# A two-layer decoder on one core: the opening's products reordered, pieces of a planned order moved, and each attention's two output halves added at once

## The chip, the cores and the metric

The kernel runs on one core of a Trainium2 chip. The metric is the time of one execution in microseconds (us) on the device; lower is better. Engines are named as in the profile: PE is TensorE (matrix products and transposes), PEld its weight loads, DVE is VectorE, ACT is ScalarE, POOL is GpSimd, SP is SyncE, which issues most of the DMA transfers. All data is float32.

## The reference

A decoder of two layers on `x` of shape (8, 256, 256): 8 sequences of 256 rows, 256 wide. Each sublayer is added to its input.

```python
x = x + L0_attn(layernorm(x))            # 16 heads of 16, rotary, biases bq bk bv bo
x = x + L0_xattn(ctx, layernorm(x), b, seq_len)   # keys and values: halves of ctx; bias b, mask by length; no projections
x = x + L0_ffn(layernorm(x))             # expert choice, see below
x = x + L1_attn(layernorm(x))            # 16 heads of 16, rotary, causal, no biases
x = x + L1_xattn(layernorm(x), ctx)      # 16 heads of 64, one learned key and value more
x = x + L1_ffn(layernorm(x))             # top-1 of 8 experts of width 704, and a shared one
```

The change touches the first four. The feed-forward of layer 0 (`B` sequences of `N` = 256 rows, `E` = 8 experts, `M` = 32 rows for each) is:

```python
t = log(clip(x @ gate_w, 1e-6))                       # (B, N, E)
for _ in range(8):                                    # Sinkhorn
    t = t - logsumexp(t, axis=-2); t = t - logsumexp(t, axis=-1)
vals, idx = top_k(swapaxes(exp(t), -1, -2), M)        # each expert chooses 32 rows of a sequence
routed = x[b, idx]                                    # gathered
out = zeros_like(x).at[b, idx].set((routed @ experts) * vals)   # a row chosen twice: one of the entries stays
```

## The kernel before

**Units and steps.** All of `x` stays in the core's memory. The first 465 us are 24 units, in the order in which they stand in the list `units`: for each pair of sequences b, b+1 of layer 0 two self attentions (units 4i and 4i+1) and two cross attentions (4i+2 and 4i+3), then the eight causal self attentions of layer 1 (units 16 to 23). A unit has four steps k, one for each half of the heads and half of the keys. Behind the units come layer 1's cross attention, its experts and the end, where the program has nothing to do with the change.

In step k of unit n the main loop issues, in this order: `scores(k + 1)` (the next step's scores: PE `st` at L334, two exps on ACT at L345, each of half the tile, and in layer 1 a causal mask on POOL for each, L350); the planned pieces marked EARLY; `values(k)` (PE `o`, L371; at odd k also the division on DVE, L387 to L397: `by_q`, `dens`, `att`, `attT`); and the other planned pieces of this step, sorted by a due number. `beside(n, k, at, piece)` puts a piece into that plan. Within these 465 us the order of each engine's instructions is this order of issue (`manual_schedule`): an instruction that waits holds all that stand behind it on its engine.

The on-chip banks for PE's results are few: one tile of four banks for the scores (so `st` waits until both exps of the step before have read it), one bank for `o`, and three banks in rotation, tag `mm`, for all else: `tr` (transposes), `qk`, `v`, `qps`/`qpsx` (queries transposed), `ao`/`oR` (outputs), `lg`, `cs`, `vps`, `cps`, `rps`, `y`, `back`.

**A self attention's pieces.** `stats` (DVE statistics, `lnrs` on POOL, L258), `norm` (`xn`, L262, on POOL; on DVE for the first two units), `rows` (four transposes `tr` of `xn` on PE, copy `xnT` on ACT, L294), `heads(0)` and `heads(1)` (`qk` for half of the rows: L282 on PE, rotary `qc`, `qs` on DVE at L402 and L418, in layer 0 the bias on POOL at L457, and for half 0 the sum `qkr` on POOL, L459), `joined` (that sum for half 1, on DVE, L463), `vals(0)`, `vals(1)` (`v` on PE, `padv` on ACT), `begin` (transposes of `qkr`, `qps`, and their copies `kT` and `qm` on ACT), and after the unit `biased` (POOL, layer 0) and `out(0)`, `out(1)`: `ao` of 128 rows in a bank of its own on PE, and an add of 256 columns to `x` on DVE (L492) each.

**A cross attention's pieces.** `vals` (POOL copies), `stats`, `norm` (`xnx`, DVE), `begin` (`qpsx` on PE at L547), `out` (`oR`, four transposes at L557, one add of 512 columns, L559).

**The expert choice.** `chosen_experts(b0, 2)` is a generator for two sequences, four of them (entries 0 to 3), and each `next` issues one piece: stats and norm (`xnb` on POOL) of both, two transposes, two gate products `lg` (with a maximum on DVE), eight rounds `cs` (column sums on PE, then five DVE operations of some 0.2 us, L661 to L668; the next round's product needs the last of them), `vps` and the search for the 32 largest (DVE), the DMAs through `slots` in memory back to `idx_row` and `by_half`, `cps` (two transposes of `by_half`, L698, a copy `col` on DVE and `pick` on POOL, L709), then for each sequence `rps` (gather as a product), `y` (experts; with `put` on POOL and L739 to L756 on DVE: two accumulations, the weight, and `ys`) and `back` (scatter as a product) with an add to `x` (L765). The tables `pieces` (entries 0 and 1), `sooner` (entry 2) and `soonest` (entry 3) say where each of them goes: (units after the pair's first, step, due number), with 4i + 4 added for entry i.

**The opening.** The first two self attentions stand before the loop. PE's order there: xn of the first transposed, its qk(0), v(0), qk(1), v(1), transposes of `qkr`, `qps`, the first `st`; then the second's transposes and qk(0), the second `st`.

**Two more rules.** `norm` of units 20 and 22 comes in step (n - 2, 1), before the `values` there, for other units of layer 1 in (n - 3, 3). In step (20, 1) POOL issues the loads of the weights of layer 1's cross attention. Behind unit 23 its outputs and the tables `wn` and `nvw` of that cross attention follow.

Of the kernel before, what the change touches and what calls it, by code (L numbers as in the profile page):

```python
# [29 lines left out]
F32 = mybir.dt.float32  # L30
# [4 lines left out]
ALU = mybir.AluOpType  # L35
# [4 lines left out]
P = 128  # L40
B, S, D = 8, 256, 256
# [16 lines left out]
PINNED = {mybir.EngineType.PE, mybir.EngineType.DVE, mybir.EngineType.Activation, mybir.EngineType.Pool, mybir.EngineType.SP}  # L58
# [99 lines left out]
def plain(  # L158
# [4 lines left out]
    nc = tc.nc  # L163
# [6 lines left out]
    x = const.tile([P, NT, D], F32, name="x")  # L170
# [90 lines left out]
    def normed(dst, src, mv, rs, i, engine=nc.vector):  # L261
        return engine.tensor_scalar(dst, src, mv[:, i, 0:1], rs[:, i : i + 1], ALU.subtract, ALU.mult)  # L262
# [11 lines left out]
    def product(out, lhsT, rhs, start, stop):  # L274
        return [
            nc.tensor.matmul(out[h], lhsT[:, h], rhs, start=start, stop=stop, skip_group_check=True)  # L276
            for h in (slice(0, 64), slice(64, P))
        ]

    def product4(out, lhsT, rhs, start, stop):  # L280
        for h in range(0, P, HP):
            nc.tensor.matmul(  # L282
                out[h : h + HP], lhsT[:, h : h + HP], rhs, start=start, stop=stop, skip_group_check=True
            )
# [114 lines left out]
    def rotary(qk, t, layer, work):  # L399

        qc = work.tile([P, 2 * H, HD], F32, tag="qc", name="qc")
        nc.vector.tensor_tensor(  # L402
            qc,
            qk.rearrange("p (h d) -> p h d", d=HD),
            cos[:, t, :].unsqueeze(1).to_broadcast([P, 2 * H, HD]),
            ALU.mult,
        )
        qs = work.tile([P, 2 * H, HD], F32, tag="qs", name="qs")
        if layer == 0:
            of = "p (h i s) -> p s h i"  # L410
            src, dst = qk.rearrange(of, s=2, i=HD // 2), qs.rearrange("p h (i s) -> p s h i", s=2)
            sn = sin0[:, t, :].rearrange("p (i s) -> p s i", s=2)
        else:
            of = "p (h s i) -> p s h i"
            src, dst = qk.rearrange(of, s=2, i=HD // 2), qs.rearrange("p h (s i) -> p s h i", s=2)
            sn = sin1[:, t, :].rearrange("p (s i) -> p s i", s=2)
        for s in range(2):
            nc.vector.tensor_tensor(  # L418
                dst[:, s],
                src[:, 1 - s],  # L420
                sn[:, s, :].unsqueeze(1).to_broadcast([P, 2 * H, HD // 2]),
                ALU.mult,
            )
        return qc.rearrange("p h d -> p (h d)"), qs.rearrange("p h d -> p (h d)")

    class SelfAttention:
# [10 lines left out]
        def norm(self):  # L437
            self.xn = work.tile([P, 2, D], F32, tag="xn", name="xn")
            for t in range(2):
                self.head = normed(  # L440
                    self.xn[:, t, :], x[:, 2 * self.b + t, :], self.mv, self.rs, t, nc.gpsimd if self.n else nc.vector
                )

        def rows(self):
# [38 lines left out]
                    xt = x[:, 2 * self.b + t, :]  # L483
                    nc.gpsimd.tensor_tensor(xt, xt, self.bias[1], ALU.add)

        def out(self, t):
            b, attT = self.b, self.core.attT
            xt = x[:, 2 * b + t, :]
            ps = mm.tile([P, 2 * D], F32, tag="mm", name="ao")[:, :D]
            for c in range(2):  # L490
                product4(ps, attT[:, c, bass.ts(t, P)], self.wo[:, c, :], c == 0, c == 1)
            nc.vector.tensor_tensor(xt, xt, ps, ALU.add)  # L492

# [5 lines left out]
    def key_tables():  # L501
        tok_i = const.tile([P, 2], I32, name="tok_i")
        nc.gpsimd.iota(tok_i, [[P, 2]], base=0, channel_multiplier=1)
        nc.vector.tensor_copy(tokid, tok_i)
        seq = const.tile([P, B], F32, name="seq")
        nc.vector.tensor_copy(seq, seq_i)
        alive = const.tile([P, B], F32, name="alive")
        nc.vector.tensor_scalar(alive, seq, 1.0, None, ALU.is_ge)
        for t in range(2):
            hid = small.tile([P, B], F32, tag="hid", name="hid")  # L510
            nc.vector.tensor_scalar(hid, seq, tokid[:, t : t + 1], -1.0e12, ALU.is_le, ALU.mult)
            nc.vector.scalar_tensor_tensor(kbias[:, :, t], hid, keyb[:, t : t + 1], alive, ALU.add, ALU.mult)
        nc.vector.tensor_tensor(
            mask2a,
            mask2.unsqueeze(1).to_broadcast([P, B, 2]),
            alive.unsqueeze(2).to_broadcast([P, B, 2]),
            ALU.mult,
        )
# [47 lines left out]
    mm = banks.enter_context(tc.tile_pool(name="amm", bufs=3, space=PSUM))  # L566
# [7 lines left out]
    def turn():  # L574
        for t in range(2):
            qc, qs = rotary(bs[:, :2, :].rearrange("p i d -> p (i d)"), t, 0, work)
            nc.vector.tensor_tensor(turned[:, t, :], qc, qs, ALU.add)
# [191 lines left out]
    units = []  # L769
# [80 lines left out]
    def beside(n, k, at, *made):  # L850
        plan.setdefault((n, k), []).append((at, made))
# [7 lines left out]
    EARLY = 0  # L859
    for n, u in enumerate(units):  # L860
        if u.__class__ is SelfAttention:
            u.n = n
            if n in (20, 22):
                beside(n - 2, 0, 80, u.stats)
                beside(n - 2, 1, EARLY, u.norm)
            else:
                beside(n - 3, 2, 80, u.stats)
                beside(n - 3, 3, EARLY, u.norm)
            beside(n - 2, 2, 30, u.rows)
            beside(n - 2, 3, 30, partial(u.heads, 0))  # L870
            beside(n - 1, 0, 30, partial(u.heads, 1))
            beside(n - 1, 1, EARLY, u.joined)
            beside(n - 1, *((2, 30) if u.layer == 0 and n % 4 else (1, 30)), partial(u.vals, 0))
            beside(n - 1, 1, 60, u.begin)
            beside(*((n, 0, 40) if u.layer else (n - 1, 2, 31) if n % 4 else (n - 1, 3, 40)), partial(u.vals, 1))
            beside(n, 3, 80, u.biased)
            for t in range(2):
                beside(n + 1, *((2 + t, 40) if u.layer else (0, 20 + t)), partial(u.out, t))
        else:
            beside(n - 1, 0, 80, u.stats, u.vals)  # L880
            beside(n - 1, 1, EARLY, u.norm)
            beside(n - 1, 1, 60, u.begin)
            beside(n + 1, *((2, 40) if n % 4 == 2 else (0, 20)), u.out)
    beside(0, 2, 40, add_up)
    beside(2, 2, 85, slot_keys)
    beside(3, 2, 50, slot_tables)

    begun = (-1, 2, 80), (0, 0, EARLY), (0, 1, 80)
    start = begun + (
        (0, 2, EARLY), (0, 3, 40), (0, 3, 41), (1, 0, 70), (1, 2, 70),  # L890
        (1, 3, 70), (2, 0, 15), (2, 1, 5), (2, 2, 10), (2, 2, 70), (2, 3, 70), (3, 0, 70), (3, 1, 45),
        (3, 2, 70), (3, 3, 85),
    )
    pieces = start + (
        (4, 1, 85), (4, 2, EARLY), (4, 3, 70), (5, 1, 10), (5, 2, 10), (5, 3, 10), (5, 3, 20), (6, 1, 10), (6, 2, 15),
    )
    sooner = start + (
        (4, 1, 84), (4, 1, 85), (4, 3, 20), (5, 0, 50), (5, 1, 35), (5, 2, 20), (5, 2, 50), (5, 3, 50), (6, 0, 50),
    )
    soonest = begun[:2] + (  # L900
        (0, 0, 80), (0, 1, EARLY), (0, 1, 65), (0, 1, 66), (0, 2, 50), (0, 2, 51),
        (0, 3, 60), (1, 0, 45), (1, 1, 10), (1, 1, 70), (1, 2, 70), (1, 3, 35), (1, 3, 70), (2, 0, 35),
        (2, 0, 70), (2, 1, 85), (2, 2, EARLY), (2, 2, 85),
        (3, 0, 10), (3, 0, 50), (3, 1, 35), (3, 2, 35), (3, 2, 50), (3, 3, 35), (4, 0, 50),
    )
    ex = [chosen_experts(2 * i, 2) for i in range(B // 2)]
    for i, made in enumerate(ex):
        for n, k, at in (pieces, pieces, sooner, soonest)[i]:
            beside(4 * i + 4 + n, k, at, partial(next, made, None))

    for u in units[:2]:
        u.n = 0
        u.stats()
        u.norm()
        if u is units[0]:
            opening = ExitStack()
            opening.enter_context(tc.issue_after(u.head.ins))
            order = ExitStack()
            order.enter_context(tc.manual_schedule(engines=PINNED))
            turn()  # L920
            u.rows()
            u.heads(0)
            u.vals(0)
            u.heads(1)
            u.joined()
            u.vals(1)
            for v in units[:2]:
                v.load()
        else:
            units[0].begin()  # L930
            units[0].core.scores(0)
            u.rows()
            u.heads(0)
            key_tables()
    for n, u in enumerate(units):
        if n == 1:
            expert_tables()
# [22 lines left out]
                wd, ctxs, wproj, wkv_x, wq_x, wout_x, nkrow, nvcol, lns, lnb = weights_x()  # L960
        opening.close()
    order.close()
    for t in range(2):
        units[-1].out(t)
    wn, nvw, hot8 = tables_x(wd, wq_x, wout_x, nkrow, nvcol)
    first.close()
    banks.close()
# [1 line left out]
    mm = banks.enter_context(tc.tile_pool(name="xmm", bufs=3, space=PSUM))  # L969
# [1878 lines left out]
```

## Time and profile before

| what | value |
|---|---|
| three executions | 1214.85, 1215.27, 1216.22 us; median 1215.27 |
| the profiled execution | 1214.46 us, of it 1212.7 us between the first and the last instruction |
| mean granted clock of PE | 0.992 of full speed |
| ACT, exps of layer 0's self and layer 1's attentions (L345) | 128 of 128 x 1024 or less, 0.917 us each |
| POOL, causal mask (L350) | 64 of 128 x 512, 0.671 us each |
| POOL, lnrs (L258) | 48, 0.732 us each |
| DVE, add of 256 columns (L492) | 0.42 us |
| DVE, add of 512 columns (L559, L765) | 0.69 us |
| xn pair on POOL (L262) | 2.42 us |
| xn pair on DVE (L262) | 0.73 to 0.86 us |

In the rows of the timeline the columns are: start in us from the beginning of the span, duration (first start to last end, where several like instructions are drawn together), engine, line, operation, output and inputs by the program's names, shape, number of instructions, and in brackets how long the engine had stood idle before it and what ended that. The granted clock is given as a share of full speed.

### The profile page before, as it was taken

What the parts mean: (1) busy time and instruction counts of PE and PEld (TensorE: products, weight loads), DVE (VectorE), ACT (ScalarE), POOL (GpSimd) and SP (SyncE); (2) the same over time, 40 slices, a digit from 0 to 9 for tenths busy, and PEclk for the clock granted to TensorE, in tenths of its full rate; (3) what the DMA queues carried; (4) which work ended last, traced back from release to release, by engine and by line L of the source; (5) the groups of instructions that cost most, each with busy time, mean ns of one, the idle gap of its engine ahead of it and who ended that gap; (6) DMA issues with size and microseconds to landing.
All of it is one profiled execution on the core that took longest, in us unless ns stands there. A gap on an engine that the chain in (4) does not pass through costs nothing.

```text
span 1212.7 us, 31559 instructions
## 1 busy us (share of the span) xinstructions
PE 1141.0 (94%) x13596; PEld 707.9 (58%) x13596; DVE 562.4 (46%) x1564; ACT 447.6 (37%) x696; POOL 417.2 (34%) x482
## 2 busy tenths in 40 slices
PE   5798989998999998999999999999999999999997
PEld 2344435444444445566666676666666486888874
DVE  4455767758775746223332433333335474222113
ACT  2666655656434361223232323232323131222220
POOL 2335344443746741132333323241416105000004
PEclk9999999999999999999999999999999999999999
DMA  7036232050200410010101010101012108599934
GB/s 223 1 127 205 91 117 91 2 171 2 83 2 11 167 71 2 18 37 18 37 19 37 18 37 19 37 19 37 19 37 72 36 2 322 217 399 404 386 123 138
DMA packets 51446, 116.76 MB, mean 96 GB/s; under 512 B 8273, under 2 KB 36417, under 8 KB 46945
## 3 DMA queue, kind: packets, MB, share of 16 engines
q1 hardware_dynamic: 45120, 98.90, 23.9%
q0 software_dynamic: 3456, 12.73, 2.9%
q10 hardware_dynamic: 2720, 3.02, 0.7%
q8 instruction: 109, 1.79, 0.6%
q14 instruction: 41, 0.33, 0.1%
HBM read 104.00 MB, written 27.93 MB: 109 GB/s over the span
## 4 chain that ended last, share of the span: by engine, by line
PE 73%; POOL 8%; DVE 7%; issue 6%; ACT 3%; DMA 2%; SPq 0%; POOLq 0%; ACTq 0%; DVEq 0%
PE h L276 7%; PE k L276 6%; PE v L276 6%; PE wo L276 5%; PE ox L1458 5%; PE stx L1419 4%; PE out L1836 4%; PE out L1653 3%; PE st L334 3%; PE h L1041 3%; PE o L371 3%; PE qk L282 3%; PE q L276 3%; PE tr L291 2%; PE fm L276 2%
## 5 line engine op out<-in xcount | busy, mean ns | idle before, releaser
L345 ACT ACTIVATE pT<-st 128x1024 f32<-128x1024 f32 (+1 forms) x128 | 110.5, 917 | 79.3 <-PE st L334 79.1
L371 PE MATMUL o<-pT,padv 128*32 128x256 f32 (+1 forms) x1536 | 100.4, 372 | 4.3 <-POOL pT L350 4.2
L1425 POOL TENSOR_TENSOR both<-pTx 128x512 f32<-128x512 f32 x64 | 82.1, 1310 | 50.5 <-issue 44.9
L371 PEld LDWEIGHTS o<-pT,padv 128*32 128x32 f32 x1536 | 40.9, 110 | 87.4 <-issue 41.7
L276 PE MATMUL h<-xrT,w 128*64 128x128 f32 (+1 forms) x1936 | 87.3, 250 | 3.1 <-issue 3.1
L276 PEld LDWEIGHTS h<-xrT,w 128*64 128x64 f32 x1936 | 84.7, 137 | 6.1 <-issue 3.9
L258 POOL TENSOR_TENSOR lnrs<-lnve,mhalf 128x2 f32<-128x2 f32 x48 | 35.1, 732 | 153.2 <-DVE lnve L256 141.8
L345 ACT ACTIVATE pT<-st,kbias 128x1024 f32<-128x1024 f32 x64 | 67.8, 1112 | 36.7 <-PE st L334 36.7
L1423 ACT ACTIVATE pTx<-stx 128x1024 f32<-128x1024 f32 x64 | 62.2, 1022 | 41.3 <-PE stx L1419 26.2
L1034 DVE TENSOR_TENSOR midr<-sl,h 128x128 f32<-128x128 f32 x102 | 29.4, 288 | 102.5 <-PE h L276 68.9
L334 PE MATMUL st<-qm,kT 32*128 32x512 f32 (+1 forms) x512 | 68.7, 606 | 5.2 <-ACT pT L345 3.3
L1033 ACT ACTIVATE sl<-h 128x128 f32<-128x128 f32 (+1 forms) x114 | 35.3, 310 | 97.8 <-PE h L276 58.8
L1419 PE MATMUL stx<-qTx,kTx 64*128 64x256 f32 x512 | 64.3, 391 | 2.5 <-ACT pTx L1423 2.5
L282 PE MATMUL qk<-l_wqkv,xnT 128*32 128x512 f32 x512 | 63.9, 616 | 2.2 <-ACT xnT L294 2.2
L1458 PE MATMUL ox<-pTx,vx 128*64 128x256 f32 x512 | 62.3, 385 | 0.0
L1513 POOL TENSOR_TENSOR oT<-oT,rs 128x512 f32<-128x512 f32 x30 | 37.3, 1274 | 66.7 <-DMA rs<-rd 66.7
L258 POOL TENSOR_TENSOR lxrs<-lxve,mhalf 128x2 f32<-128x2 f32 x8 | 5.6, 702 | 154.3 <-DVE sc L1172 123.3
L1419 PEld LDWEIGHTS stx<-qTx,kTx 64*128 64x128 f32 x512 | 46.1, 186 | 20.3 <-ACT pTx L1423 7.2
L276 PE MATMUL wo<-wout_x,oT 128*64 128x256 f32 x512 | 58.0, 379 | 0.0
L350 POOL TENSOR_SCALAR_AFFINE_SELECT pT<-pT 128x512 f32<-128x512 f32 x64 | 42.1, 671 | 39.3 <-ACT pT L345 39.3
L1458 PEld LDWEIGHTS ox<-pTx,vx 128*64 128x64 f32 x512 | 33.9, 136 | 26.4 <-issue 12.1
L1466 DVE COPY oT<-ox 128x512 f32<-128x512 f32 x16 | 11.1, 691 | 81.0 <-PE ox L1458 81.0
(361 smaller groups left out, 2195.1 us busy)
## 6 DMA issues: line engine op xcount, KB each, us to landing
w<-packs SPq DMA_DIRECT2D x22, 1408.0 KB
w<-packs SPq DMA_DIRECT2D x22, 768.0 KB
rs<-rd SPq DMA_DIRECT2D x16, 512.0 KB
packs<-L_ffn_w_eDF SPq DMA_DIRECT2D x8, 704.0 KB
packs<-L_ffn_w_eDF SPq DMA_DIRECT2D x8, 640.0 KB
packs<-L_ffn_w_eFD SPq DMA_DIRECT2D x8, 640.0 KB
ctxT<-ctx_T SPq DMA_DIRECT2D x8, 512.0 KB
wkv_x<-L_xattn_Wkv POOLq DMA_DIRECT2D x1, 4096.0 KB, 14.0
```

Of the source, the lines that this page charges most:

```text
L258: nc.gpsimd.tensor_tensor(rs[:, :n], ve[:, :n], mhalf[:, :n], ALU.pow)
L276: nc.tensor.matmul(out[h], lhsT[:, h], rhs, start=start, stop=stop, skip_group_check=True)
L282: nc.tensor.matmul(out[h : h + HP], lhsT[:, h : h + HP], rhs, start=start, stop=stop, skip_group_check=True)
L334: nc.tensor.matmul(st[:, r, :, :n], self.kT[rows, c, bass.ts(kt, P)], self.qm[rows, :, c, q0:], start=True, stop=True,)
L345: nc.scalar.activation(pT[:, :, :, :n], st[:, 2 * k : 2 * k + 2, :, :n], AF.Exp, scale=self.scale, **kb)
L350: nc.gpsimd.affine_select(out=pT[:, :, :, :P], in_=pT[:, :, :, :P], compare_op=ALU.is_ge, fill=0.0, base=0, pattern=[[0, 2], [0, 2], [1, P ...
L371: nc.tensor.matmul(o[HP * j : HP * j + HP, m, q0:], self.v_pad[:, kt, 8 * c + 2 * j + m, :], pTs[j // 2][:, j % 2, m, : S - q0], start=kt ...
L1419: nc.tensor.matmul(st[:, g, kt, :], kT[rows, c, bass.ts(kt, P)], qT[rows, c, :], start=True, stop=True)
L1423: nc.scalar.activation(pT, st, AF.Exp, scale=scale)
L1425: nc.gpsimd.tensor_tensor(both, pT[:, :, 0, :], pT[:, :, 1, :], ALU.add)
L1458: nc.tensor.matmul(o[XD * g : XD * (g + 1), i, :], v[:, kt, 2 * (c2 + i) + g, :], pT[:, g, kt, :], start=kt == 0, stop=kt == 1, skip_group ...
L1836: nc.tensor.matmul(ps[h], mid[:, i, h], sets[k % len(sets)][1][:, i, :], start=i == 0, stop=i == NFC - 1, skip_group_check=True,)
```

## The change

Five things are done.

1. *Opening.* PE's order becomes: xn of the first transposed, qk(0), v(0), qk(1), xn of the second transposed, v(1), transposes of the first's `qkr`, `qps`, qk(0) of the second, `st`, `st`. DVE's and POOL's order there stays.
2. *`SelfAttention.out`.* Both halves are written to one bank, and one add of 512 columns follows. In layer 1 both stand where the first one stood, in step (n + 1, 2); in layer 0 where both stood, in (n + 1, 0).
3. *Places of units' pieces.* `out` of every second cross attention goes behind heads(1) of the coming unit, in the same step; `rows` in layer 1 goes from due number 30 to 60 of its step.
4. *Table entries.* norm0 of entries 0 to 2 goes from (0, 0, EARLY) to (0, 1, EARLY), behind `joined` there. In `pieces`, `cps` goes from (4, 3) to (5, 0) and the last `back` from (6, 2) to (6, 3). In `sooner` and `soonest` several pieces go a fraction of a step or a step back.
5. *`norm` of units 20 and 22* runs on DVE in place of POOL.

The calls of `load` for the first two units that go with the old opening did nothing (they load from the third sequence on).

```diff
@@ SelfAttention.norm
-                    ..., nc.gpsimd if self.n else nc.vector
+                    ..., nc.gpsimd if self.n not in (0, 1, 20, 22) else nc.vector
@@ SelfAttention.out
-        def out(self, t):
-            b, attT = self.b, self.core.attT
-            xt = x[:, 2 * b + t, :]
-            ps = mm.tile([P, 2 * D], F32, tag="mm", name="ao")[:, :D]
-            for c in range(2):
-                product4(ps, attT[:, c, bass.ts(t, P)], self.wo[:, c, :], c == 0, c == 1)
-            nc.vector.tensor_tensor(xt, xt, ps, ALU.add)
+        def out(self):
+            attT, xb = self.core.attT, x[:, 2 * self.b : 2 * self.b + 2, :]
+            ps = mm.tile([P, 2, D], F32, tag="mm", name="ao")
+            for t in range(2):
+                for c in range(2):
+                    product4(ps[:, t, :], attT[:, c, bass.ts(t, P)], self.wo[:, c, :], c == 0, c == 1)
+            nc.vector.tensor_tensor(xb, xb, ps, ALU.add)
@@ the plan
-            beside(n - 2, 2, 30, u.rows)
+            beside(n - 2, 2, 60 if u.layer else 30, u.rows)
...
-            for t in range(2):
-                beside(n + 1, *((2 + t, 40) if u.layer else (0, 20 + t)), partial(u.out, t))
+            beside(n + 1, *((2, 40) if u.layer else (0, 20)), u.out)
...
-            beside(n + 1, *((2, 40) if n % 4 == 2 else (0, 20)), u.out)
+            beside(n + 1, *((2, 40) if n % 4 == 2 else (0, 40)), u.out)
...
-    begun = (-1, 2, 80), (0, 0, EARLY), (0, 1, 80)
+    begun = (-1, 2, 80), (0, 1, EARLY), (0, 1, 80)
...
     pieces = start + (
-        (4, 1, 85), (4, 2, EARLY), (4, 3, 70), (5, 1, 10), (5, 2, 10), (5, 3, 10), (5, 3, 20), (6, 1, 10), (6, 2, 15),
+        (4, 1, 85), (4, 2, EARLY), (5, 0, 60), (5, 1, 10), (5, 2, 10), (5, 3, 10), (5, 3, 20), (6, 1, 10), (6, 3, 10),
     )
     sooner = start + (
-        (4, 1, 84), (4, 1, 85), (4, 3, 20), (5, 0, 50), (5, 1, 35), (5, 2, 20), (5, 2, 50), (5, 3, 50), (6, 0, 50),
+        (4, 1, 84), (4, 1, 85), (5, 0, 20), (5, 0, 50), (5, 1, 35), (5, 2, 50), (5, 3, 10), (5, 3, 60), (6, 0, 50),
     )
-    soonest = begun[:2] + (
-        (0, 0, 80), (0, 1, EARLY), (0, 1, 65), (0, 1, 66), (0, 2, 50), (0, 2, 51),
-        (0, 3, 60), (1, 0, 45), (1, 1, 10), (1, 1, 70), (1, 2, 70), (1, 3, 35), (1, 3, 70), (2, 0, 35),
+    soonest = (-1, 2, 80), (0, 0, EARLY), (0, 0, 80), (0, 1, EARLY)
+    soonest += (
+        (0, 2, 35), (0, 2, 36), (0, 3, 10), (0, 3, 50),
+        (1, 0, 10), (1, 0, 70), (1, 1, 35), (1, 1, 70), (1, 2, 70), (1, 3, 35), (1, 3, 70), (2, 0, 35),
         (2, 0, 70), (2, 1, 85), (2, 2, EARLY), (2, 2, 85),
-        (3, 0, 10), (3, 0, 50), (3, 1, 35), (3, 2, 35), (3, 2, 50), (3, 3, 35), (4, 0, 50),
+        (3, 0, 70), (3, 1, 50), (3, 2, 35), (3, 3, 10), (3, 3, 35), (4, 0, 10), (4, 0, 50),
     )
@@ the opening
-    for u in units[:2]:
-        u.n = 0
-        u.stats()
-        u.norm()
-        if u is units[0]:
...
-            u.rows()
-            u.heads(0)
-            u.vals(0)
-            u.heads(1)
-            u.joined()
-            u.vals(1)
...
-        else:
-            units[0].begin()
-            units[0].core.scores(0)
-            u.rows()
-            u.heads(0)
-            key_tables()
+    first_u, second_u = units[:2]
+    first_u.stats()
+    first_u.norm()
...
+    first_u.rows()
+    first_u.heads(0)
+    first_u.vals(0)
+    first_u.heads(1)
+    first_u.joined()
+    second_u.stats()
+    second_u.norm()
+    second_u.rows()
+    first_u.vals(1)
+    first_u.begin()
+    second_u.heads(0)
+    first_u.core.scores(0)
+    key_tables()
```

More of the change, by code (lines that the diff above doesn't have):

```diff
@@ L440, in norm @@
                 self.head = normed(
-                    self.xn[:, t, :], x[:, 2 * self.b + t, :], self.mv, self.rs, t, nc.gpsimd if self.n else nc.vector
+                    self.xn[:, t, :], x[:, 2 * self.b + t, :], self.mv, self.rs, t, nc.gpsimd if self.n not in (0, 1, 20, 22) else nc.vector
                 )
@@ L909, in plain @@
             beside(4 * i + 4 + n, k, at, partial(next, made, None))
-    for u in units[:2]:
-        u.n = 0
-        u.stats()
-        u.norm()
-        if u is units[0]:
[L916 to L920, printed above, removed]
-            u.rows()
-            u.heads(0)
-            u.vals(0)
-            u.heads(1)
-            u.joined()
-            u.vals(1)
-            for v in units[:2]:
-                v.load()
-        else:
-            units[0].begin()
-            units[0].core.scores(0)
-            u.rows()
-            u.heads(0)
-            key_tables()
+    first_u, second_u = units[:2]
+    first_u.stats()
+    first_u.norm()
+    opening = ExitStack()
+    opening.enter_context(tc.issue_after(first_u.head.ins))
+    order = ExitStack()
+    order.enter_context(tc.manual_schedule(engines=PINNED))
+    turn()
+    first_u.rows()
[11 more added lines that the diff above has]
+    key_tables()
     for n, u in enumerate(units):
@@ L962, in plain @@
     order.close()
-    for t in range(2):
-        units[-1].out(t)
+    units[-1].out()
     wn, nvw, hot8 = tables_x(wd, wq_x, wout_x, nkrow, nvcol)
```

## The prediction

> **What bounds the kernel now.** I read the page's busy shares, slices and chain of waits first, then TensorE's waits by releaser up to 465 us, then the timeline around each place that the diff touches.
>
> ```profile
> PE 1141.0 (94%) x13596; PEld 707.9 (58%) x13596; DVE 562.4 (46%) x1564; ACT 447.6 (37%) x696; POOL 417.2 (34%) x482
> ...
> PE   5798989998999998999999999999999999999997
> ...
> PE 73%; POOL 8%; DVE 7%; issue 6%; ACT 3%; DMA 2%; SPq 0%; POOLq 0%; ACTq 0%; DVEq 0%
> ```
>
> PE is the bound, 94% busy. One slice is 30.3 us; the change ends with the attentions, at about 465 us, in the 16th slice. Behind that the order is the old one and PE has 9 in all slices but the last, so whatever is won or lost before 465 us arrives whole at the end. It can only come from PE's idle time, and that stands here:
>
> ```profile
> PE st L334 <- ACT pT L345: 8.5, 8, 1.5
> PE tr L291 <- DVE xn L262: 7.9, 1, 7.9
> PE tr L291 <- DVE qkr L463: 7.8, 7, 1.7
> PE cps L698 <- DMA by_half<-slots: 6.8, 3, 2.9
> PE qpsx L547 <- DVE xnx L262: 4.3, 4, 1.1
> PE o L371 <- POOL pT L350: 4.2, 5, 1.6
> PE back L282 <- DVE ys L756: 3.0, 2, 1.5
> ```
>
> Columns: total us, times, longest. A wait of PE costs more than its length:
>
> ```profile
> 171.60 0.32 PE L698 MATMUL cps<-ident,by_half 4*128 4x4 f32 x2 [2.16 <-DMA by_half<-slots]
> 171.73 2.10 PE L334 MATMUL st<-qm,kT 32*128 32x512 f32 x8
> 173.76 1.68 PE L371 MATMUL o<-pT,padv 128*32 128x256 f32 x16
> ...
> 303.19 1.97 PE L371 MATMUL o<-pT,padv 128*32 128x256 f32 x16 [1.62 <-POOL pT L350]
> 305.09 1.12 PE L557 MATMUL oR<-ident,attT 128*128 128x128 f32 x4
> 306.13 2.90 PE L282 MATMUL qk<-l_wqkv,xnT 128*32 128x512 f32 x16
> ```
>
> After 2.16 us of waiting the st takes 2.10 instead of 1.14 (as st at 28.25 below) and o 1.68 instead of 1.07: 1.57 lost beyond the wait. After 1.62 us (303.19) o, oR and qk lose 0.90 + 0.46 + 1.00 = 2.4 against their usual 1.07, 0.66 and 1.90. In both places the granted clock of the 10 us is 0.83. After the 1.68 us before cps at 375.38 and the 1.48 before back at 204.13 nothing slows. So I price a new PE wait of 2 us or more at its length plus 1.6, bounds 0 and 2.4.
>
> **The change, part by part** (plus is slower; the sum is made on the profiled execution, 1214.46 us).
>
> *Opening.* PE's old order: qk and v of the first attention, its qkr transposes and qps, st(0), then the second's transposes of xn and its qk. In the new one the transposes of the second's xn stand before v(1). DVE's order is unchanged, and it makes that xn last:
>
> ```profile
> 21.53 0.73 DVE L262 TENSOR_SCALAR xn<-x,lnmv,lnrs 128x256 f32<-128x256 f32 x2 [0.82 <-POOL lnrs L258]
> ...
> 21.76 2.09 PE L334 MATMUL st<-qm,kT 32*128 32x512 f32 x8 [1.41 <-ACT qm L313]
> ...
> 28.25 1.14 PE L334 MATMUL st<-qm,kT 32*128 32x512 f32 x8
> ```
>
> PE, which began v(1) at 16.41, now waits from about there to 21.9, some 5.4 us; v(1), the qkr transposes and qps are queued behind the waiting transposes. From 22.3: half a pair of transposes 0.5, v(1) at half clock 1.9, four qkr transposes 1.0, qps 0.6, the second's qk 1.9: st(0) at 28.2 (was 21.76). Its first exps no longer lie behind qk, so st(1) follows them: 1.14 + 1.94 later, 31.4 against 28.25, +3.15. The second's rotary is ahead, though, so the 1.50 us that PE waited for its qkr at 36.05 mostly goes: −1.2. **+1.9**; bounds +0.5 (v, transposes and qps keep full clock, 1.45 less) and +3.5 (nothing regained).
>
> *Outputs in one bank.* PE does the same products. DVE adds 512 columns once (0.69, by the row of L559) instead of 0.42 twice, but the chain add, statistics, lnrs, xnx, qpsx now begins with 0.69 in place of the last 0.42: +0.27 at the four places where PE waits for xnx (52.01, 66.54, 113.11, 127.87; 1.0 to 1.1 each): **+1.1**. In the third and fourth group rps or y products lie between and hide it; uncovered it would be 1.1 more, which is the upper bound; −0.6 the lower, if two freed semaphores and a bank do more than that.
>
> *Cross output behind heads(1), norm0 behind joined.* POOL's xnb pair (2.42) no longer stands before the rotary's bias add (L457, 1.27) of the unit's second half, which PE awaits through qkr: waits of 0.57 (98.02), 1.36 (161.67) and 1.34 (235.51) go: **−3.3**, bounds 0 and −3.3. Late next would be the xnb transposes; their place is a step or more away.
>
> *cps one step later.* Table entries 0 and 1: cps moves from just before st at 171.73 and 246.32 to behind that unit's o and ao, four us on. by_half, issued at 169.19, landed at about 171.6, well before that. Gone are 2.16 + 1.57 and 2.92 + 1.69 (st 1.75, o 1.94, ao 2.12 there against 1.14, 1.07, 1.91); cps itself, formerly hidden in the wait, adds 0.13 each: **−8.1**. Behind cps on its engines, col (DVE) and pick (POOL, 1.84) have until rps, one step later. The lower bound of the gain is 6.8 − 1.7 = 5.1, the two waits alone; the upper 8.3.
>
> *back1 one step later.* PE's 1.48 us for ys goes, at 204.13 and 278.80. But back's 1.93 us were also what covered the next chain: cs4 (206.58) needs five DVE operations (1.1 us) of the cs3 round, which queue on DVE behind the two accumulations, weight and ys up to 204.3. Without back, PE passes the four transposes and stands from 203.25 until 205.6, about 2.3 us. By the order of the rows heads(0) then starts at 209.4 instead of 208.79, and back adds its bit behind: +0.85 each, **+1.7** for both, bounds −2 and +3.
>
> *Layer 1 (units 16 to 23).* Entry 2's y0, rps and back and entry 3's pieces move half a step to a step; rows come later. Two waits arise: rps0 for pick, which POOL does behind L459 and both masks (326.2 to 328.25, 2.05), and in unit 17 cs for a chain that now stands behind y0's DVE work (335.5 to 337.4, 1.9). Two go: POOL xn of units 20 and 22 (0.93 each at 365 and 411; the pair is 2.42 on POOL, 0.73 to 0.86 on DVE), and most of the 1.68 at cps, 375.38. By the rows PE is 2.5 early at 404.5. In unit 21 POOL is rid of xn of 22 before the weight triggers, PE gets to st(21.1) at 413.4 instead of 419.33, but its o then waits for POOL's own stream (lnrs 0.73, masks 1.24, xn of 23 2.48, three lnrs 2.02, L459 1.27, masks 1.68): 421.6 instead of 425.59. Net **−4.0**, bounds −6 (POOL free, st's gain kept) and +1.5 (both waits longer, gain at 375 lost).
>
> *End.* ao doubled before st(23.0) delays exp by 0.62; the last add and nvw come 0.5 sooner: **+0.1**, bounds −1 and +1.
>
> Sum: 1.9 + 1.1 − 3.3 − 8.1 + 1.7 − 4.0 + 0.1 = −10.6.
>
> *Clock after the new waits.* cs4 twice (2.3 us; 0.7 x 1.6 = 1.1 each), rps0 and cs in layer 1 (2.0; half of 1.6 each), o of unit 21 (3 us, 1.3 since POOL binds there): 2.2 + 1.6 + 1.3 = **+5.1**.
>
> Result −5.5: 1209.0 on the profiled execution. That execution stands 0.8 below the median of 1215.27, so **1209.8 us**.
>
> [...]
>
> **Rivals.**
> (a) *No clock loss.* The same waits, but none of the five falls so that the clock drops. For it: 1.48 and 1.68 us cost nothing; against it: 2.16, 2.92 and 1.62 all did. 1215.27 − 10.6 = 1204.7.
> (b) *Wash.* The gain at the xnb places and in layer 1 is half, the rest as forecast: PE just meets the next chain (the o that waits for POOL's masks, five times now, 4.2 us). −5.5 + 1.65 + 2.0 = −1.9, and +1.6 if the opening regains nothing: 1213.4 to 1215.0.
> (c) *Slower: clock drops eat the gain.* The five new waits each cost 2.4 beyond their length, as after 303.19 (+12.0), and the opening reaches its upper bound (+1.6): −10.6 + 13.6 = +3.0, 1218.3. It decides from 2.1 per wait on (10.6 : 5), with the opening as forecast. Against it: four waits out of five would have to meet the dearer row.
> (d) *The change doesn't remove the DMA wait*: by_half is late again, because SP issues it after more transfers. In the trace slots' reads go out ahead of memk, and the order on SP isn't touched. The two waits' 5.1 on the forecast: 1214.9.
>
> **How the numbers follow.** Two executions of this kernel can be told apart from about 0.2% (2.4 us) on; that puts "the same" at 1212.8 to 1217.7. Chances: forecast 0.42 (1206.5 to 1212.5), (a) 0.18, (b) 0.14, (c) 0.20, (d) 0.06. Faster: 0.40 of the forecast, all of (a) and 0.02 of (b), 0.60. The same: 0.02 of the forecast, 0.12 of (b) and all of (d), 0.20. Slower: (c), 0.20. The range reaches a little beyond (a)'s time at the bottom and to (c)'s at the top, and leaves out the farther halves of both, 0.19: 1203.5 to 1218.3; the forecast's own is 1206.5 to 1212.5.
>
> **What would show it.** cps without a wait for by_half in units 9 and 13, and the following st at 1.14; a wait of some 5 us of PE for xn at 16.5 and st(1) near 31; cs waiting about 2.3 us for g in units 10 and 14; no wait at the qkr transposes of units 5, 9, 13; o of unit 21 waiting for POOL. I am wrong if the opening loses more than 3.5 us, if cps merely waits at its new place, or if the 10-us windows around the new cs waits show clocks of 0.83 more often than three times.

## The result: no change, and the profile after

The changed kernel takes 1215.03 us (median of 12, 1212.86 to 1217.11), the kernel before, beside it, 1215.74 (12 runs, 1208.77 to 1219.43). The ratio is 1.0002, with a 95% interval of 0.9989 to 1.0014 (the quotient of the two medians is 0.9994; either says that nothing changed). The forecast of 1209.8 is refuted in what it said: nothing was gained. The profiled execution of the changed kernel has a span of 1211.1 us at a granted clock of 0.988; before it was 1212.7 at 0.992.

First TensorE's waits up to 465 us, in the changed kernel (releaser; total us, times, longest):

```profile
PE tr L291 <- DVE xn L262: 13.1, 2, 7.6
PE st L334 <- ACT pT L345: 10.7, 8, 2.1
PE cs L282 <- DVE g L668: 8.6, 8, 2.2
PE qpsx L547 <- DVE xnx L262: 5.7, 4, 1.5
PE ao L282 <- DVE attT L397: 3.8, 1, 3.8
PE o L371 <- POOL pT L350: 3.5, 4, 1.6
PE o L371 <- DVE by_q L387: 3.2, 3, 1.2
PE tr L291 <- DVE qkr L463: 1.6, 3, 0.9
```

The waits that were to go are gone: `by_half` (6.8 before) and `ys` at `back` (3.0) stand nowhere, `qkr` fell from 7.8 to 1.6. Others are in their place, and the total hardly moved (56.4 us before, 56.0 now, up to 470 us): the second xn in the opening (+5.2), `cs` for g (8.6 against 1.1), `xnx` (5.7 against 4.3), `by_q` (3.2, new), `attT` at the end (3.8 against 2.2).

Two places, in the timeline of PE. The opening, then units 10 and 11:

```profile
20.54 1.09 PE L291 MATMUL tr<-ident,xn 128*128 128x128 f32 x4 [5.51 <-DVE xn L262]
21.56 1.93 PE L282 MATMUL v<-l_wqkv,xnT 128*32 128x256 f32 x16
23.42 1.11 PE L291 MATMUL tr<-ident,qkr 128*128 128x128 f32 x4
24.33 1.06 PE L475 MATMUL qps<-ident,qkr 128*128 128x128 f32 x4
25.32 1.94 PE L282 MATMUL qk<-l_wqkv,xnT 128*32 128x512 f32 x16
27.19 1.14 PE L334 MATMUL st<-qm,kT 32*128 32x512 f32 x8
30.39 1.14 PE L334 MATMUL st<-qm,kT 32*128 32x512 f32 x8 [2.06 <-ACT pT L345]
...
203.52 0.42 PE L282 MATMUL cs<-g,ones 128*32 128x16 f32 x16 [2.24 <-DVE g L668]
203.86 2.09 PE L334 MATMUL st<-qm,memk 32*128 32x512 f32 x8
205.88 1.94 PE L371 MATMUL o<-pT,padv 128*32 128x256 f32 x16
207.59 2.96 PE L282 MATMUL back<-ys,put 128*32 128x256 f32 x32
210.38 1.89 PE L282 MATMUL qk<-l_wqkv,xnT 128*32 128x512 f32 x16
```

PE waits 5.5 us in the opening, and v at 21.56 takes 1.93 where it took 1.04. The `cs` wait of 2.24 is followed by st 2.09 for 1.14, o 1.94 for 1.07, back 2.96 for 1.9; the granted clock from 203 to 209 us is 0.50. Such products are called half speed below.

A table made of such rows is the tool of this study. It shows how much later (+) or earlier (-) the first `st` of a step starts than in the kernel before, in us, for one profiled execution of each kernel; the experiments are told below.

| step | changed | gains only | layer 0 one bank | layer 0 one bank, two adds | layer 1 one bank | all but outputs |
|---|---|---|---|---|---|---|
| 0.3 (36.85 us) | +1.12 | -2.32 | -2.36 | -0.08 | +0.13 | +0.96 |
| 3.0 (70.75) | +2.70 | -2.32 | -0.92 | +1.56 | +0.13 | +0.97 |
| 9.0 (166.27) | +1.11 | -4.68 | -2.45 | +1.00 | -2.20 | -1.34 |
| 10.0 (185.89) | -2.36 | -8.14 | -5.92 | -1.65 | -5.67 | -4.81 |
| 11.1 (210.73) | +1.58 | -8.14 | -4.01 | -0.70 | -5.67 | -4.17 |
| 14.0 (260.55) | -4.37 | -13.97 | -9.97 | -5.71 | -11.49 | -10.12 |
| 16.0 (297.07) | -3.39 | -13.95 | -9.55 | -4.76 | -11.48 | -7.89 |
| 23.0 (445.87) | -1.62 | -13.46 | -9.50 | -4.30 | -4.87 | -9.95 |

In the changed kernel the first column falls where the forecast said (9.0 to 10.0: 3.5; 11.1 to 14.0: 6.0) and climbs in between and behind. Which part of the change makes it climb was to be tried.

### The profile page after: what moved, and what is told of

It is laid out like the page before. It is cut to its first block, busy times and chain, and to the rows that moved or that the text cites. A ratio compares the mean times of both kernels' runs of the same rounds, so it can differ in the third digit from the quotient of the medians.

```text
span 1211.1 us, 31526 instructions
## 1 busy us (share of the span) xinstructions
PE 1140.6 (94%) x13596; PEld 712.1 (59%) x13596; DVE 568.0 (47%) x1552; ACT 448.4 (37%) x696; POOL 415.4 (34%) x478
## 4 chain that ended last, share of the span: by engine, by line
PE 77%; POOL 7%; DVE 6%; issue 6%; ACT 4%; DMA 1%; SPq 0%; POOLq 0%; ACTq 0%; DVEq 0%
PE h L276 7%; PE k L276 6%; PE v L276 6%; PE wo L276 5%; PE ox L1454 5%; PE st L334 4%; PE stx L1415 4%; PE o L371 4%; PE out L1832 4%; PE out L1649 3%; PE qk L282 3%; PE h L1037 3%; PE q L276 3%; ACT pT L345 2%; PE tr L291 2%
## 5 line engine op out<-in xcount | busy, mean ns | idle before, releaser
L1462 DVE COPY oT<-ox 128x512 f32<-128x512 f32 x16 | 11.1, 691 | 81.0 <-PE ox L1454 81.0
```

## The experiments

All were timed in five rounds beside the kernel before; ratios are to it, with their intervals.

**1. The last back early again**, in the changed kernel:

```diff
-        ..., (6, 1, 10), (6, 3, 10),
+        ..., (6, 1, 10), (6, 2, 15),
```

> The changed kernel with one thing undone: the last back of entries 0 and 1 again in step (6, 2) instead of (6, 3). Theory (the moved back uncovers the Sinkhorn chain, so cs waits 2.2 us in units 10 and 14, and the half clock after the first of these costs 2.8 more): cs no longer waits, the 1.48 us before back returns, st of step 11.1 follows that of 10.2 by 15.2 us as in the kernel before instead of 19.1, and the time is 2 to 5 us under the changed kernel's, about 1211. Rival (the clock drops in any case after one of these waits, 1.5 or 2.2 alike): the rows move, the time stays at 1215.

1212.32 us, 0.9986 (0.9969 to 1.0003). The `cs` wait of 2.2 is gone and the one for `ys` is back:

```profile
203.49 1.93 PE L282 MATMUL back<-ys,put 128*32 128x256 f32 x32 [1.49 <-DVE ys L756]
205.35 0.66 PE L291 MATMUL tr<-ident,xn 128*128 128x128 f32 x4
205.94 0.32 PE L282 MATMUL cs<-g,ones 128*32 128x16 f32 x16
206.18 1.14 PE L334 MATMUL st<-qm,memk 32*128 32x512 f32 x8
207.25 1.07 PE L371 MATMUL o<-pT,padv 128*32 128x256 f32 x16
```

Nothing runs slow here. In unit 14 of this execution it was the other way round: st 1.48 behind the `ys` wait, 1.9 lost. The ratios differ by some 2 us, but their intervals overlap (0.9969 to 1.0003 here, 0.9989 to 1.0014 for the changed kernel), so the time alone doesn't show the gain. By the rows the stretches from 10.3 to 11.1 and from 14.3 to 15.1 lose 0.4 and 1.9 here against 3.9 and 1.0 in the changed kernel. It is a small part at most.

**2. cps alone one step later**, in the kernel before:

```diff
-        (4, 1, 85), (4, 2, EARLY), (4, 3, 70), (5, 1, 10), ...
+        (4, 1, 85), (4, 2, EARLY), (5, 0, 60), (5, 1, 10), ...
```

> The kernel before with one thing of the change: cps of entries 0 and 1 one step later. Theory (the by_half wait was on the path and nothing takes its place): 3.5 us less in unit 9 and 4.3 in unit 13 by the rows, about 8 us under the kernel before, 1207.5. Rival (the path behind it is set by DVE or the transfers, which catch up by unit 10): the lead at unit 9 is gone by unit 11 and the time is 1213 or more.

1207.22 us, 0.9941 (0.9918 to 0.9963): 7.2 of the 8.1 forecast, and the rows show 3.5 at unit 9 and 4.3 at unit 13. The wait for `by_half` did not move; it vanished.

**3. Layer 1 as before**, in the changed kernel: the old tables of entries 2 and 3, rows at 30 and the norm of units 20 and 22 on POOL; the single outputs stay.

> The changed kernel with entries 2 and 3, the norm of units 20 and 22 and the rows of layer 1 as before. Theory (the new order in units 16 to 21 lost 1.0 us by the rows instead of gaining 4): about 1 us under the changed kernel, 1214. Rival (my forecast: the new order gains 4 and only this execution's clock hid it): 3 to 4 us over it, 1218.5.

1219.35 us, 1.0040 (1.0023 to 1.0056): 4 to 5 us slower than the changed kernel, so my theory fell and its rival held. The new order is worth 4 to 5 us. Yet the rows of the changed kernel lose 1.8 between 16.0 and 23.0. Something else in layer 1 had to cost more than the order gains, and in this kernel only the outputs were left: from 16.0 to 23.0 it loses 7.0.

**4. Only the parts that removed waits**, in the kernel before:

```diff
-        (4, 1, 85), (4, 2, EARLY), (4, 3, 70), ...
+        (4, 1, 85), (4, 2, EARLY), (5, 0, 60), ...
-    begun = (-1, 2, 80), (0, 0, EARLY), (0, 1, 80)
+    begun = (-1, 2, 80), (0, 1, EARLY), (0, 1, 80)
-            beside(n + 1, *((2, 40) if n % 4 == 2 else (0, 20)), u.out)
+            beside(n + 1, *((2, 40) if n % 4 == 2 else (0, 40)), u.out)
```

> The kernel before with three things of the change that removed waits by the rows: cps of entries 0 and 1 later, norm0 of entries 0 to 2 behind joined, the output of every second cross attention behind heads(1). Theory (each gain is real and all others of the change give it back): 8 + 3.5 us under the kernel before, about 1204. Rival (the gains are bound to the other parts): 1210 or more.

1202.12 us, 0.9902 (0.9872 to 0.9931): 12 us faster. By the rows 11.1 us lie between 0.3 and 23.0 (second column of the table). This is the base for what follows. It was not timed again beside experiments 5 to 12; each is compared with it through the kernel before, and since the base's interval is wide, a difference between two such ratios stands within some 4 us (an estimate from the intervals).

**5. Layer 1's new order on that base**, with the outputs in halves (the lines of `sooner`, `soonest`, `rows` and the norm of units 20 and 22, as in the change's diff):

> The run of the three gains alone (1202.1) with the change's order for entries 2 and 3, rows of layer 1 and the norm of units 20 and 22 added; outputs stay in two halves. Theory (that order is good by itself, as the forecast had it, and what spoils layer 1 is the single output): 2 to 4 us under it by the rows between steps 16.0 and 23.0, about 1199. Rival (the order only mends what the single output breaks): no gain or 1 to 3 us over it, 1203 to 1205.

1200.13 us, 0.9880 (0.9865 to 0.9895). By the rows 2.1 us are gained between 16.0 and 23.0, where the base lost 0.5. The intervals of the two overlap; it is not shown to be faster than the base. It has the lowest median of the study, nearly 15 us below the kernel before and the changed one.

**6. Layer 1's outputs in one bank**, on the base of 4:

```diff
-            for t in range(2):
-                beside(n + 1, *((2 + t, 40) if u.layer else (0, 20 + t)), partial(u.out, t))
+            if u.layer:
+                beside(n + 1, 2, 40, u.out_both)
+            else:
+                for t in range(2):
+                    beside(n + 1, 0, 20 + t, partial(u.out, t))
...
-    for t in range(2):
-        units[-1].out(t)
+    units[-1].out_both()
```

`out_both` is the changed kernel's `out`: both halves in one bank, one add.

> The run of the three gains alone (1202.1) with layer 1's outputs in one bank and one add in step (n + 1, 2). Theory (the second half of ao, 0.86 us of products, was the cover of waits in step 3: for by_half, by_q, xn and POOL's masks): +6 to +7 between steps 16.0 and 23.0, 1208.5. Rival (the run with layer 1's old order lost there through clock drops alone): +1 or less, 1203.

1209.36 us, 0.9955 (0.9942 to 0.9968): 0.9955 - 0.9902, or 6.4 us, slower. The rows: -11.48 at 16.0, -4.87 at 23.0. The same place in the base and here:

```profile
357.51 1.05 PE L282 MATMUL ao<-l_wo,attT 128*32 128x256 f32 x16
...
361.71 0.28 PE L698 MATMUL cps<-ident,by_half 4*128 4x4 f32 x2 [1.51 <-DMA by_half<-slots]
361.93 1.92 PE L282 MATMUL qk<-l_wqkv,xnT 128*32 128x512 f32 x16
```

```profile
356.51 1.93 PE L282 MATMUL ao<-l_wo,attT 128*32 128x256 f32 x32
...
366.11 0.28 PE L706 MATMUL cps<-ident,by_half 4*128 4x4 f32 x2 [2.36 <-DMA by_half<-slots]
366.32 3.20 PE L282 MATMUL qk<-l_wqkv,xnT 128*32 128x512 f32 x16
```

The second half of `ao` is 0.86 us of products (1.91 us for both, 1.05 for one) that stood in step 3. Without it PE comes that much sooner to what it waits for next: the wait for `by_half` grows by just that, from 1.51 to 2.36. Here half speed follows as well: qk takes 3.20 for 1.92, and the granted clock from 340 to 370 us is 0.95, against 1.00 in the base. From step 16.0 on PE waits 19.8 us in the base and 24.8 here, so most of the 6.4 is waiting. From the waits between 290 and 470 us, first in the base:

```profile
...
PE o L371 <- POOL pT L350: 2.5, 4, 1.0
PE st L334 <- ACT pT L345: 2.2, 2, 1.5
PE ao L282 <- DVE attT L397: 2.2, 1, 2.2
PE tr L291 <- POOL xn L262: 1.9, 4, 0.8
PE cps L698 <- DMA by_half<-slots: 1.5, 1, 1.5
PE tr L291 <- DVE qkr L463: 1.4, 2, 0.9
```

and with the outputs in one bank:

```profile
PE ao L282 <- DVE attT L397: 3.8, 1, 3.8
PE o L371 <- POOL pT L350: 3.3, 4, 1.6
PE st L334 <- ACT pT L345: 3.1, 2, 1.5
...
PE cps L706 <- DMA by_half<-slots: 2.4, 1, 2.4
PE tr L291 <- DVE qkr L463: 2.3, 2, 1.3
...
PE cs L282 <- DVE g L676: 1.8, 1, 1.8
PE o L371 <- DVE by_q L387: 1.1, 2, 0.9
```

**7. Layer 0's outputs in one bank**, on the base of 4 (one bank, one add of 512 in step (n + 1, 0); layer 1 in halves):

> The run of the three gains alone (1202.1) with layer 0's outputs in one bank and one add. Theory: each of the four waits for xnx grows by 0.3 to 0.4, +1.5 up to unit 7, nothing in units 9 to 14, 1203.7; with one clock drop, as in the changed kernel at step 2.3, 1204.5. Rival (the larger of the waits, 1.5 instead of 1.1, drop the clock more often than not): +4, 1206.

1209.63 us, 0.9949 (0.9931 to 0.9966): 0.0047, 5.7 us, slower; the rival's size. The waits for `xnx` grew as forecast:

```profile
64.22 0.84 PE L547 MATMUL qpsx<-ident,xnx 128*128 128x128 f32 x4 [1.12 <-DVE xnx L262]
64.99 1.14 PE L334 MATMUL st<-qm,memk 32*128 32x512 f32 x8
66.06 1.07 PE L371 MATMUL o<-pT,padv 128*32 128x256 f32 x16
```

is the base, and here it is

```profile
64.96 0.84 PE L555 MATMUL qpsx<-ident,xnx 128*128 128x128 f32 x4 [1.51 <-DVE xnx L262]
65.73 1.25 PE L334 MATMUL st<-qm,memk 32*128 32x512 f32 x8
66.91 1.94 PE L371 MATMUL o<-pT,padv 128*32 128x256 f32 x16
```

The four waits grew by 1.4 in all, from 4.3 to 5.7, and two `cs` waits of 0.44 in units 10 and 14 came up, for a chain that is 0.4 later: 2.3 by waiting. The rest is put down to the clock, which is argued and only in part shown. In this execution the wait of 1.51 is followed by half speed (o 1.94), as it is in the changed kernel; the waits of 1.49 and 1.48 are not, nor is the same wait of 1.51 in experiments 1 and 3. None of the base's four waits of 1.0 to 1.1 for `xnx` is. The profiled execution was the kernel's fastest: two of the six took 1204.1 and 1204.3 us at granted clocks of 0.993 and 0.994, four took 1209.6 to 1210.8 at 0.988 and 0.989, and where those four lost it no trace shows. The mean clock is 0.9903 over the six and 0.9937 over the base's six; 0.0034 of 1208 us is 4.1 us, as an estimate, and 3.4 are left to explain.

**8. The opening alone**, on the base of 4: the change's order before the loop.

> The run of the three gains alone (1202.1) with the change's opening. Theory (PE waits 5.5 us for the second's xn, and its clock halves): step 0.3 comes 1 to 3.5 us later than in the kernel before, and 3.5 to 5.5 us later than in the run of the three gains, whose opening met full clock; time about 1204 to 1205. Rival (the wait is regained by step 0.3, since the second's rotary is ahead): within 1 us, 1202 to 1203.

1203.16 us, 0.9905 (0.9891 to 0.9919): not to be told from the base. PE waits 5.52 us for the second's xn, and step 0.3 comes 1.68 later than in the kernel before and 4.0 later than in the base, as the theory had it; its time lies nearer to the rival's. But the opening differs from execution to execution: step 0.3 lay between -2.5 and +0.2 with the old order in the nine profiled executions (mean -1.0; the products there ran at full or at half speed, the first `st` in 1.14 us in the base and in 2.09 in the kernel before), and between +1.0 and +3.3 with the new in five (mean +1.9).

**9. One bank, two adds** in layer 0, for the add's length:

```diff
             for t in range(2):
                 for c in range(2):
                     product4(ps[:, t, :], ...)
-            nc.vector.tensor_tensor(xb, xb, ps, ALU.add)
+                nc.vector.tensor_tensor(xb[:, t, :], xb[:, t, :], ps[:, t, :], ALU.add)
```

> The run with layer 0's outputs in one bank (1209.6), but with an add of 256 for each half in place of one of 512. Theory (the longer add behind the last product delays the statistics, xnx and so qpsx by 0.3 to 0.4, and the waits of 1.5 drop the clock): the four waits for xnx are back at 1.0 to 1.1, the cs waits of 0.44 in units 10 and 14 are gone, time 1202 to 1203.5. Rival (the shared bank makes the first add wait for both halves): the waits stay at 1.5 or grow, 1209.

1209.22 us, 0.9949 (0.9931 to 0.9967). The theory's row is right and its time wrong:

```profile
46.84 1.05 PE L282 MATMUL ao<-l_wo,attT 128*32 128x256 f32 x16
48.51 1.07 PE L282 MATMUL ao<-l_wo,attT 128*32 128x256 f32 x16 [0.61 <-DVE x L500]
...
52.75 0.84 PE L555 MATMUL qpsx<-ident,xnx 128*128 128x128 f32 x4 [1.10 <-DVE xnx L262]
```

The `xnx` wait is back at 1.10, but PE, as the program is built, doesn't write the bank's second half until DVE has read the first (the add runs from 48.03 to 48.45, the second `ao` starts at 48.51): eight waits of 0.61 to 0.72, 5.2 in all. So the longer add does delay xnx (waits of 1.49, 1.51, 1.23 and 1.48 in experiment 7, of 1.10, 1.12, 0.92 and 1.09 here), and in this program a bank's first half is not read while its second is written. Of the three ways that ran, only two banks with two adds had neither these waits nor the longer ones for `xnx`.

**10. Layer 1's halves at once, but in two banks:**

```diff
-                beside(n + 1, *((2 + t, 40) if u.layer else (0, 20 + t)), partial(u.out, t))
+                beside(n + 1, *((2, 40 + t) if u.layer else (0, 20 + t)), partial(u.out, t))
```

> The run of the three gains alone (1202.1) with both halves of layer 1's outputs in step (n + 1, 2), but each in its bank with its add. Theory (what costs in layer 1 is the place: the second half's 0.86 us no longer cover waits in step 3): the same +6 between steps 16.0 and 23.0 as with one bank, 1208 to 1209. Rival (the bank and the longer add cost it): within 1.5 us of 1202.

1209.24 us, 0.9955 (0.9940 to 0.9969), the same loss as in 6, and the rows lose 6.3 us between 16.0 and 23.0. `cps` waits 2.53, and the qk behind it takes 1.92: this time full speed follows. From step 16.0 on PE waits 24.3 us. In layer 1 it is the place, not the bank or the add.

**11. Layer 1's outputs in one bank, in step 3:**

```diff
-                beside(n + 1, 2, 40, u.out_both)
+                beside(n + 1, 3, 40, u.out_both)
```

> The run with layer 1's outputs in one bank (1209.4), but in step (n + 1, 3) instead of (n + 1, 2). Theory (place): step 3 has its cover back and twice as much, step 2 loses 0.86 us of it, where fewer waits end: 1 to 4 us under it, 1205 to 1208. Rival (the bank and the add): no change, 1209.

1202.26 us, 0.9894 (0.9879 to 0.9910): better than expected, nothing is lost against the base. `cps` waits 0.88, the waits for `cs` and `by_q` are gone, and from step 16.0 on PE waits 20.0 us, as in the base (19.8). With 6 and 10 this settles layer 1: the same bank and add, one step later, cost nothing that shows.

**12. The changed kernel with its outputs in halves**, at the old places in both layers:

> The changed kernel with only its outputs undone: two banks, two adds, at the old places in both layers. Theory (the outputs take back 11 to 12 us, all else of the change gains that): 1202 to 1204. Rival (the effects found by single steps are not additive, the clock evens them out): 1209 or more.

1204.54 us, 0.9918 (0.9903 to 0.9934), half a us above the theory's range: undoing the outputs alone gives 10 us back (1.0002 - 0.9918 = 0.0084), and the intervals of the two are far apart.

## Why the forecast was wrong

Experiments 4, 5, 12 and the changed kernel contain each other, so they add up the change by time (ratio to the kernel before, times 1215):

| added | ratio | step |
|---|---|---|
| cps, norm0, cross output behind heads(1) | 0.9902 | -11.9 |
| layer 1's order, norm of units 20 and 22 | 0.9880 | -2.7 |
| opening, last back one step later | 0.9918 | +4.6 |
| outputs in one bank, added at once | 1.0002 | +10.2 |

- *cps, -8.1:* right. 7.2 by time alone, and by the rows 3.5 and 4.3.
- *norm0 and the cross output, -3.3:* right. The rows show 3.8 in the changed kernel, a little more than the bound of 3.3 (4.0 to 5.0: 0.76; 8.0 to 9.0: 1.54; 12.0 to 13.0: 1.54).
- *Opening, +1.9:* the mechanism is the one forecast, with a wait of 5.5 and 27.19 for the first `st` (forecast 28.2). Between +1.0 and +3.3 by the rows against the one execution of the kernel before, 2.9 between the means of experiment 8; the time alone doesn't resolve it.
- *Last back, +1.7, and its part of the clock, 2.2:* the wait was forecast as 2.3 and measured 2.24 and 2.19. One of the two was followed by half speed. By the rows +3.9 and +1.0 (10.3 to 11.1 and 14.3 to 15.1), 4.9 against a forecast of 3.9; by time some 2, which experiment 1 doesn't resolve.
- *Layer 1, -4.0, less 2.9 for clock:* the order by itself gained: 4.6 by time in the changed kernel (experiment 3), 2.7 on the base, where the intervals overlap. The term didn't ask what the outputs' new place does there. With it the profiled execution loses 1.8.
- *Outputs in one bank, +1.1, bounds -0.6 and +2.2:* this is the step that failed. "PE does the same products" was true and was the wrong question. In layer 1 half of these products left step 3, where they covered part of the waits that end in or behind it (in experiment 6 those for `by_half`, `qkr`, g, `by_q` and `attT` grew); on the base that cost 6.4 (experiments 6, 10 and 11). I named the cover where back was moved, and didn't ask it of `ao`. In layer 0 the four longer waits were forecast rightly (1.1; measured 1.4). The third and fourth group, which I took to be hidden, show two `cs` waits of 0.44, and an effect of these waits on the clock wasn't priced at all: I priced it at five waits of about 2 us and more, while in experiment 7 half speed followed a wait of 1.5. Layer 0's outputs cost 5.7 on the base, of which 2.3 are waits that the trace shows. Together the outputs cost 10.2 in the changed kernel instead of 1.1 (by the rows of one execution each, against experiment 12, 4.3 from step 0.3 to 16.0 and 3.8 from there to 23.0). With this one term in place the forecast would have read 1219.
- *Clock after the new waits, +5.1:* of the five waits the two in units 10 and 14 came as forecast, rps0 waited 1.08 + 0.26 instead of 2.05, the 1.9 of unit 17 came as 1.51 at `qps` and 0.42 at `cs`, and o of unit 21 waited 1.32 + 0.18 for POOL instead of 3. The loss of clock can't be told for each. Without the outputs' term the forecast is -6.6, and experiment 12 measures -10.0: the other terms together were 3.4 too dear, which offsets a part of the miss by luck. Which of them were, no run separates.
- *End, +0.1:* the rows agree from step 23.3 on, which starts 1.63 earlier, as the span ends 1.6 earlier.

How much of the outputs' 10 us is clock: the profiled executions of the changed kernel and of experiment 12 differ by 9.1 us of span. PE waits 4.4 us longer in the first up to 470 us (56.0 against 51.6). The 4.7 that are left fit the granted clocks, 0.988 and 0.992 (0.004 of 1210 us is 4.8). So about half is clock, as an estimate.

Of the rivals (b), the wash, has the right time by the wrong cause: xnx and layer 1's order didn't give half, the outputs took all. (c) named a part of the mechanism, clock behind new waits, but put it at other waits. (d) is refuted by experiment 2. (a), no loss of clock, is contradicted by the rows behind 203.52, and nothing was gained.

The length of a single wait doesn't tell in these runs whether half speed follows: products ran at half speed behind waits of 1.51 (experiment 7 and the changed kernel) and 2.24 (the changed kernel), and at full speed behind others of 1.48 (experiment 7), 1.51 (experiments 1 and 3), 2.19 (the changed kernel) and 2.53 (experiment 10). In the changed kernel o ran at half speed (1.94 at 363.72) behind a wait of 1.17 for `by_q`, with one of 0.93 for `qkr` 2.7 us before it. The same wait in the same place, the 1.51 for `xnx`, is followed by half speed in one execution and by full speed in another; what decides it no run here shows.

## What to carry to other kernels

Before moving a product off a step, list what waits in that step and what of it the product covered: the engine does the same work, but the work was a cover (0.86 us of `ao` in experiment 6, whose loss let the wait for `by_half` grow from 1.51 to 2.36). In layer 0 two results that are drained one after the other were best in two banks (1202.1 us); one bank with one long read delayed what follows (waits for `xnx` of 5.7 instead of 4.3 us, 1209.6), and one bank with two reads held up the writer (eight waits, 5.2 us, 1209.2). In layer 1, in a step with room for it, one bank cost nothing that shows (1202.3 in experiment 11). Where half speed can follow a wait, as it did behind one of 1.51 us in experiment 7, small delays at many places can take back what a few large waits won: the outputs cost 10 us, and the two waits for `by_half` had been worth 7.

## What the runs showed of the hardware beyond that

One program's executions differ by several us, and the clock goes with it. The kernel before ran 25 times beside experiments 1 to 4: the three executions with a granted clock of 0.994 to 0.996 took 1208.3 to 1208.7 us, the two with 0.986 took 1218.0 and 1218.2; the 2.4 us from which on the forecast told two executions apart were too few. From 0.994 to 0.986 a share of 0.008 of the clock is lost; taken over 1213 us that makes 9.7 us, as an estimate. The clock doesn't explain every spread: experiment 1's kernel took 1209.7 us at 0.988 and 1213.9 at 0.989. A single profiled execution can therefore be several us off its kernel's median (1204.1 against 1209.6 in experiment 7), and rows of two executions should be compared place by place, where durations show whether the clock had dropped, rather than by their ends.
